# Bringing four experts' results back as two float32r parts in two rounds of products

## The chip, the cores and the metric

The kernel runs on one core of a Trainium2 chip. The metric is the device time of one execution in microseconds (us), lower is better. A program that runs on one core has its five engines work side by side: PE multiplies matrices (PEld in a profile is its loading of weights, which overlaps), DVE and ACT do elementwise work, POOL does some elementwise work and issues the indirect transfers, and SP issues the other transfers. Each engine, and each queue of transfers, goes through its own instructions in the order of the program and waits on semaphores for the others.

## The reference

The input is 16 sequences (b) of 512 tokens with 128 features. Six blocks follow one another, each added to x:

```python
x = x + 0.5 * L0_ffn(layernorm(x))     # a small network per feature
x = x + L0_attn(layernorm(x))          # causal attention, 16 heads of width 8
x = x + 0.5 * L0_ffn(layernorm(x))
x = x + 0.5 * L1_ffn(layernorm(x))     # experts, first pass: k=0
x = x + L1_attn(layernorm(x))          # a linear recurrence over the tokens
x = x + 0.5 * L1_ffn(layernorm(x))     # experts, second pass: k=1
```

The expert block is what the change touches. Each of 8 experts picks the 128 tokens of a sequence that score highest for it, runs them through two products with a gelu between, multiplies each row by that token's gain g, and adds the rows to the tokens that they came from:

```python
scores = einsum('ntd,ed->nte', x, gate_w)
g, m = top_k(softmax(scores).transpose(0, 2, 1), 128)    # gains and tokens, per sequence and expert
h = gelu(einsum('nekd,edf->nekf', x[batch, m], w1))      # 128 x 512 per sequence and expert
h = einsum('nekf,efd->nekd', h, w2)                      # 128 x 128
out = zeros_like(x).at[batch, m].add(g[..., None] * h)   # back to the tokens
```

## The kernel before

The kernel is one long program for all 16 sequences. The order on PE, ACT, DVE and POOL is written out by hand: Python generators each emit a few instructions and yield, and one main loop steps them. One step of that loop is called a turn. `turn()` emits what stands in the list `later` (work that was put off by one turn, mostly reads of a product's result), then steps the generators in `urgent` and `sides`. Until about 960 us the turns go through the attention of the sequences; in the background run the L0 networks.

Then `experts()` becomes the main generator. It goes through a list `order` of 256 jobs, a job being one expert's 128 tokens of one sequence in one of the two passes k. In the same turns there run in the background: `fetch` (POOL gathers a job's 128 rows with an indirect transfer xg, L864), `dispatch` (PE transposes two jobs at a time into ps_x, L888, ACT or DVE copies them to xin, L890), `recurrences` (two sequences at a time: norm with L286 to L303 and ps_t L317, ps_f L1051, ps_l L1060, ps_u L1070, scans L1074, ps_h L1090, and the scores ps_g L749), `routing` (picking 128 tokens of 512 for 64 rows at once: 16 rounds of three DVE instructions, L795 to L799), and `back`.

Results go back in two ways. Experts 0 to 3 of every sequence, and all eight of the last sequence in the last pass, go by products: 132 jobs. The other 124 go by transfer. `order` takes the jobs by products and the jobs by transfer alternately, the latter at a distance of some jobs behind, so that a sequence's four jobs by transfer come after its four jobs by products.

The loop keeps the last four jobs in `line`; each round of the loop emits something for each of them and has three yields, so a job takes three turns. For a job:

- In its own round, PE makes the hidden values ps_h (L939, four float32 products of 128 columns, which the profile shows as eight instructions) and ACT takes the gelu (L941) into one of four slots `hs`.
- One round later (`line[1]`), PE makes ps_y (L954, again eight instructions) and ACT multiplies by the gains (L957).
- For a job by products, DVE makes `sels` (L951), a 128x512 matrix in bfloat16 with a one where a row's token number equals the column. The scaled result is split into three bfloat16 parts whose sum is the float32 value: `yes[..0]` by ACT (L957), the remainder `rest` in float32 by DVE (L963), `yes[..1]` by ACT one round later (L945), `yes[..2]` by DVE (L960).
- Three rounds later (`line[3]`), PE multiplies the selection with the parts: for each of the four chunks of 128 tokens, three products of 128 columns into `acc` (L972), which is one bank of PSUM and collects four jobs. After the fourth, one add on DVE (L976) puts the bank on x[b], and one transfer on SP writes x[b] to a place in memory, `sums[k, b]` (L982).
- For a job by transfer, the scaled result stands in `ye`, and two rounds after its own (`line[2]`) POOL issues an indirect transfer that adds the rows to `sums[k, b]` in memory (L986). After a sequence's last one, `back` waits 18 turns and reads the sum back into x[b] (L923) for the recurrence, or copies it to the output in the last pass (L928). In the first pass it counts the sequence as done 9 turns later, and a pair of done sequences lets the next recurrence begin.

The tiles `mo` and `ye` are two buffers of 20 KB per partition that the attention no longer needs; the slots named above are cut from them.

Of the kernel before, what the change touches and what calls it, by code (L numbers as in the profile page):

```python
# [8 lines left out]
F32 = mybir.dt.float32  # L9
U32 = mybir.dt.uint32  # L10
BF16 = mybir.dt.bfloat16
F16 = mybir.dt.float16
AF = mybir.ActivationFunctionType
ALU = mybir.AluOpType
AX = mybir.AxisListType

P = 128
S = 512
NT = S // P
D = 128  # L20
# [11 lines left out]
E = 8  # L32
# [6 lines left out]
EP = 4  # L39
# [7 lines left out]
def tile_macaron(  # L47
# [9 lines left out]
    nc = tc.nc  # L57
    B = x_in.shape[0]
# [5 lines left out]
    x = []  # L64
# [34 lines left out]
    with ExitStack() as ph:  # L99
# [796 lines left out]
        def experts():  # L896

            mo = ptp.tile([P, 10, S], F32, name="mo", tag="pt")
            hs = [mo[:, i, :].rearrange("p (f j) -> p f j", f=NF) for i in range(4)]

            rest = [mo[:, 4, bass.ts(i, D)] for i in range(4)]

            def half(i, dtype):
                return mo[:, i // 2, i % 2 * (S // 2) : (i % 2 + 1) * (S // 2)].bitcast(dtype)

            sels = [half(14 + i, BF16) for i in range(4)]
            yes = [half(i, BF16)[:, 0 : 3 * D].rearrange("p (i d) -> p i d", i=3) for i in (12, 13, 18, 19)]  # L910

            iota = half(10, F16)
            nc.gpsimd.iota(mo[:, 6, :], pattern=[[1, S]], base=0, channel_multiplier=0,
                           allow_small_or_imprecise_dtypes=True)
            nc.gpsimd.tensor_copy(iota, mo[:, 6, :])
            ye = ptp.tile([P, 10, S], F32, name="ye", tag="pt")
            sums, line, acc = {}, [None] * 4, None
# [12 lines left out]
            while begun[0] < len(order) or any(line):  # L930
                now = None
                if begun[0] < moved[0]:
                    i = begun[0]
                    now = order[i] + (i % 4,)
                    k, b, e, u = now
                    begun[0] += 1
                    pst = scp.tile([P, NF, CAP], F32, name="ps_h", tag="ps_sc")
                    for f in range(NF):
                        nc.tensor.matmul(pst[:, f, :], lhsT=mw1[e][:, bass.ts(f, P)],  # L939
                                         rhs=xins[i // E % 2][:, i % E, :], start=True, stop=True)  # L940
                    nc.scalar.activation(hs[u], pst, AF.Gelu)  # L941
                prod = [work is not None and by_product(*work[:3]) for work in line]
                if prod[2]:
                    u = line[2][-1]
                    nc.scalar.copy(yes[u][:, 1, :], rest[u])  # L945
                yield
                if line[1]:
                    k, b, e, u = line[1]
                    g, n = b // GB, (b % GB) * E + e
                    if prod[1]:  # L950
                        nc.vector.tensor_scalar(sels[u], iota, tokT[g][:, n : n + 1], None, ALU.is_equal)  # L951
                    py = stp.tile([CAP, D], F32, name="ps_y", tag="ps_st")
                    for f in range(NF):
                        nc.tensor.matmul(py, lhsT=hs[u][:, f, :], rhs=mw2[e][:, f, :],  # L954
                                         start=(f == 0), stop=(f == NF - 1))
                    yu = yes[u][:, 0, :] if prod[1] else ye[:, b % 2 * (E - EP) + e - EP, 0:D]
                    nc.scalar.activation(yu, py, AF.Copy, scale=gainT[g][:, n : n + 1])  # L957
                if prod[2]:
                    v = line[2][-1]
                    nc.vector.tensor_sub(yes[v][:, 2, :], rest[v], yes[v][:, 1, :])  # L960
                yield
                if prod[1]:
                    nc.vector.scalar_tensor_tensor(rest[u], in0=py, scalar=gainT[g][:, n : n + 1],  # L963
                                                   in1=yes[u][:, 0, :], op0=ALU.mult, op1=ALU.subtract)
                if prod[3]:
                    k, b, e, u = line[3]
                    last = E - 1 if (k, b) == (1, B - 1) else EP - 1
                    if e == 0:
                        acc = avp.tile([P, NT, D], F32, name="acc", tag="ps_av")
                    for c in range(NT):  # L970
                        for w in range(3):
                            nc.tensor.matmul(acc[:, c, :], lhsT=sels[u][:, bass.ts(c, P)], rhs=yes[u][:, w, :],  # L972
                                             start=(e == 0 and c == 0 and w == 0), stop=(e == last and w == 2),
                                             skip_group_check=True)
                    if e == last:
                        nc.vector.tensor_add(x[b], acc, x[b])  # L976
                        if last < E - 1:
                            sums[k, b] = tc.dram_tile([S, D], F32, name=f"sum{k}_{b}")
                            to = sums[k, b].rearrange("(c p) d -> p c d", p=P)
                        else:  # L980
                            to = out[b].rearrange("(c p) d -> p c d", p=P)
                        nc.sync.dma_start(out=to, in_=x[b])  # L982
                if line[2] and not prod[2]:
                    k, b, e, u = line[2]
                    g, n = b // GB, (b % GB) * E + e
                    nc.gpsimd.indirect_dma_start(  # L986
                        out=sums[k, b], out_offset=bass.IndirectOffsetOnAxis(ap=tokI[g][:, n : n + 1], axis=0),
                        in_=ye[:, b % 2 * (E - EP) + e - EP, 0:D], in_offset=None, compute_op=ALU.add,
                    )
# [252 lines left out]
```

## Time and profile before

| | |
|---|---|
| median of 4 runs | 1663.89 us |
| lowest and highest | 1659.38, 1667.8 us |
| the profiled execution | 1667.7 us |
| its span in the profile | 1665.9 us |
| granted clock of PE over the span | 0.981 |
| PE busy | 1552.2 us (93%) |
| PE weight loads busy | 1078.3 us (65%) |
| DVE busy | 1136.3 us (68%) |
| ACT busy | 1001.9 us (60%) |
| POOL busy | 1021.7 us (61%) |
| products of L972 | 1584, 117.3 us busy |
| adding transfers of L986 | 124, 201.5 us busy on POOL |

The span runs from the first instruction of the program to the last; the execution's own time is 1.8 us longer. Matmuls are pipelined, so the mean duration of one is longer than its distance from the next, and the chain of waits, which follows the end of the program back through whatever released each step, gives the price of one more. A share of busy time is an average over stages with different limits, so stages are read one by one. POOL's time for an indirect transfer is that of issuing it; the transfer itself follows.

### The profile page before, as it was taken

Reading aid. Unit: us, or ns where it says so; the run is one execution under the profiler, and the core shown is the slowest. Engines: PE = TensorE matmul, PEld = TensorE weight load, DVE = VectorE, ACT = ScalarE, POOL = GpSimd, SP = SyncE. Lnnn points to the kernel's source line nnn. Section 1 sums busy time; section 2 is a strip of 40 time slices with the busy share of each in tenths; the row PEclk is TensorE's granted clock in tenths of the full one; section 3 lists DMA queues with packets and bytes.
Section 4 is the critical chain, followed back from the end, with each engine's and each line's share of the span. In section 5 each row is a group of like instructions: output and inputs, shape, how many; then the busy total and the mean of one; then the engine's idle time right before and its main releaser. Section 6 shows DMA issues by size and latency. Waiting matters only on the chain.

```text
span 1665.9 us, 35158 instructions
## 1 busy us (share of the span) xinstructions
PE 1552.2 (93%) x12813; PEld 1078.3 (65%) x12813; DVE 1136.3 (68%) x3616; ACT 1001.9 (60%) x2016; POOL 1021.7 (61%) x1486
## 2 busy tenths in 40 slices
PE   5689999999999999999989899999999999999998
PEld 2234445445444444454544489989988999889998
DVE  6588878888888888889987235964479555842222
ACT  3346677787778776777776754444443454444444
POOL 2634556556755665556543757667765777767774
PEclk9779999999999999999999999999999999999999
DMA  4110110111101110111122123223323333333332
GB/s 126 65 65 24 53 57 30 39 47 57 43 33 41 57 52 17 46 58 42 33 80 72 30 47 73 62 58 74 69 63 66 68 73 67 66 64 66 74 68 55
DMA packets 103253, 94.91 MB, mean 57 GB/s; under 512 B 13230, under 2 KB 91639, under 8 KB 102839
## 3 DMA queue, kind: packets, MB, share of 16 engines
q1 hardware_dynamic: 76220, 67.72, 13.1%
q0 software_dynamic: 26048, 24.93, 9.4%
q8 instruction: 101, 1.65, 0.4%
q14 instruction: 74, 0.60, 0.1%
q10 hardware_dynamic: 810, 0.02, 0.0%
HBM read 59.07 MB, written 37.49 MB: 58 GB/s over the span
## 4 chain that ended last, share of the span: by engine, by line
PE 69%; DVE 18%; ACT 4%; issue 3%; POOL 3%; DMA 1%; SPq 0%; DVEq 0%; ACTq 0%; POOLq 0%
PE ps_h L939 12%; PE ps_y L954 12%; PE ps_av L696 7%; PE ps_st L673 6%; PE ps_sc L610 6%; DVE below L615 5%; PE acc L972 5%; PE ps_kg L364 3%; PE ps_s L337 3%; PE ps_t L317 3%; DVE ln_st L286 2%; ACT pt L676 2%; PE ps_x L888 2%; PE ps_ko L385 2%; PE ps_g L749 1%
## 5 line engine op out<-in xcount | busy, mean ns | idle before, releaser
L678 POOL TENSOR_SCALAR_AFFINE_SELECT pt<-pt 128x128 f32<-128x128 f32 (+2 forms) x704 | 252.5, 366 | 327.9 <-ACT pt L676 323.1
L676 ACT ACTIVATE pt<-ps_st 128x512 f32<-128x512 f32 x682 | 368.2, 563 | 94.9 <-PE ps_st L673 89.2
L615 DVE CUSTOM_DVE_ANT_0 below<-ps_sc,causal 128x512 bf16<-128x512 f32 (+1 forms) x512 | 315.7, 617 | 80.2 <-PE ps_sc L610 64.9
L941 ACT ACTIVATE mo<-ps_h 128x512 f32<-128x512 f32 x256 | 152.7, 597 | 247.0 <-PE ps_h L939 134.0
L864 POOL DMA_INDIRECT xg<-xnd,tokI x256 | 250.5, 979 | 77.0 <-issue 45.2
L939 PE MATMUL ps_h<-xin,mw 128*128 128x128 f32 x2048 | 279.8, 279 | 0.8 <-issue 0.5
L954 PE MATMUL ps_y<-mw,mo 128*128 128x128 f32 x2048 | 274.6, 276 | 4.5 <-DVE mo L963 2.7
L610 PE MATMUL ps_sc<-kp,qp 72*128 72x512 bf16 (+3 forms) x1024 | 260.2, 306 | 11.7 <-DVE maxs L615 6.6
L673 PE MATMUL ps_st<-qp,kp 99*128 99x512 bf16 x992 | 250.7, 304 | 16.8 <-ACT pt L676 16.2
L986 POOL DMA_INDIRECT sum<-ye,tokI x124 | 201.5, 1625 | 90.6 <-ACT ye L957 39.7
L939 PEld LDWEIGHTS ps_h<-xin,mw 128*128 128x128 f32 x2048 | 251.4, 193 | 7.4 <-issue 6.1
L954 PEld LDWEIGHTS ps_y<-mw,mo 128*128 128x128 f32 x2048 | 250.9, 192 | 8.1 <-DVE mo L963 3.4
L673 PEld LDWEIGHTS <-kp 99*128 99x128 bf16 x1024 | 94.7, 100 | 177.1 <-issue 159.6
L370 ACT ACTIVATE kan_h<-kan_s,rbias,kw 128x512 f32<-128x512 f32 x256 | 205.9, 813 | 4.8 <-PE ps_kg L364 4.8
L696 PE MATMUL ps_av<-pt,va 128*32 128x512 f32 (+3 forms) x2048 | 164.6, 439 | 0.0
L620 DVE TENSOR_REDUCE maxs<-ps_sc 128x2 f32<-128x512 f32 (+1 forms) x192 | 130.3, 686 | 35.2 <-PE ps_sc L610 34.8
L610 PEld LDWEIGHTS <-qp 72*128 72x128 bf16 x1024 | 96.6, 100 | 79.9 <-issue 57.3
L960 DVE TENSOR_TENSOR mo<-mo 128x128 bf16<-128x128 f32 x132 | 38.4, 291 | 139.0 <-ACT mo L945 116.8
L972 PE MATMUL acc<-mo 128*128 128x128 bf16 x1584 | 117.3, 220 | 12.7 <-ACT mo L945 5.7
L972 PEld LDWEIGHTS <-mo 128*128 128x128 bf16 x1584 | 101.4, 99 | 31.2 <-issue 29.8
L696 PEld LDWEIGHTS ps_av<-pt,va 128*32 128x32 f32 x2048 | 53.5, 109 | 93.6 <-issue 43.1
L293 POOL TENSOR_TENSOR ln_rstd<-ln_rstd,mhalf 128x4 f32<-128x4 f32 x96 | 101.0, 1052 | 8.0
(194 smaller groups left out, 2341.3 us busy)
## 6 DMA issues: line engine op xcount, KB each, us to landing
qp<-qs SPq DMA_DIRECT2D x64, 288.0 KB
xnd<-kan_x SPq DMA_DIRECT2D x32, 256.0 KB
sum<-x SPq DMA_DIRECT2D x31, 256.0 KB
qs<-qpart SPq DMA_DIRECT2D x48, 128.0 KB
kp<-ks SPq DMA_DIRECT2D x48, 96.0 KB
x<-in_L_attn_x_dram SPq DMA_DIRECT2D x16, 256.0 KB
mw<-in_L_ffn_w_dram SPq DMA_DIRECT2D x16, 256.0 KB
xg<-xnd,tokI POOLq DMA_INDIRECT x256
```

Of the source, the lines that this page charges most:

```text
L370: nc.scalar.activation(h, sk[half], AF.Relu, bias=rbias[:, half, v : v + 1], scale=kw1[:, half, v : v + 1])
L610: nc.tensor.matmul(v[:, u, 0:n], lhsT=qp[r][0 : 9 * HD, g, bass.ts(c, P)], rhs=kp[0 : 9 * HD, r, 0:n], start=alone, stop=(u == len(gs) - 1 ...
L615: nc.vector.tensor_tensor_reduce(below[:, 0:n], v[:, 0, 0:n], causal[:, S - n : S], 1.0, LOWEST, ALU.add, ALU.max, accum_out=maxs[:, c, h ...
L673: nc.tensor.matmul(v[:, u, 0:n], lhsT=kp[ROWS, r, bass.ts(c, P)], rhs=qp[r][ROWS, g, c * P : S], start=True, stop=True)
L676: nc.scalar.activation(o, v[:, :, 0:n], AF.Exp, scale=HD ** -0.5)
L678: nc.gpsimd.affine_select(out=dg, in_=dg, compare_op=ALU.is_ge, fill=0.0, base=0, pattern=[[0, len(gs)], [1, P]], channel_multiplier=-1)
L696: nc.tensor.matmul(po[32 * g : 32 * g + 32, c * P : S], lhsT=va[:, c, r, :], rhs=pt[:, g, OFF[c] : OFF[c] + n], start=(c == 0), stop=(c == ...
L864: nc.gpsimd.indirect_dma_start(out=xgs[i // E % 2][:, i % E, :], out_offset=None, in_=xnd[b], in_offset=bass.IndirectOffsetOnAxis(ap=tokI[ ...
L939: nc.tensor.matmul(pst[:, f, :], lhsT=mw1[e][:, bass.ts(f, P)], rhs=xins[i // E % 2][:, i % E, :], start=True, stop=True)
L954: nc.tensor.matmul(py, lhsT=hs[u][:, f, :], rhs=mw2[e][:, f, :], start=(f == 0), stop=(f == NF - 1))
L972: nc.tensor.matmul(acc[:, c, :], lhsT=sels[u][:, bass.ts(c, P)], rhs=yes[u][:, w, :], start=(e == 0 and c == 0 and w == 0), stop=(e == las ...
L986: nc.gpsimd.indirect_dma_start(out=sums[k, b], out_offset=bass.IndirectOffsetOnAxis(ap=tokI[g][:, n : n + 1], axis=0), in_=ye[:, b % 2 * ( ...
```

## The change

The jobs by products no longer use three bfloat16 parts. The result is kept as two parts in float32r, a 4-byte type that PE takes in place of float32: the value as ACT writes it in that type, and the remainder as DVE writes it. The selections are float32r too. The products of four experts are no longer spread over their four rounds of the loop: when the fourth job has come to `line[3]`, two entries are put on the list `rounds`, and each round of the loop takes one. Such a round makes one half of the tokens (two chunks): for each chunk and each of the four experts one product of 256 columns, 128 for each of the two parts, into a bank that is laid out as chunk, part, feature. In the next turn DVE adds the two parts to that half of x[b], one after the other, and SP writes that half to memory.

The cast L945 and the subtraction L960 go away. Selections and parts have eight slots instead of four; the float32 results of the jobs by transfer move to another tile, and two buffers of the attention's pool `va` take some of the parts. A job by transfer now issues its adding transfer at `line[3]`, one round later than before. For the last sequence in the last pass, eight jobs go by products in two groups of four, and only the second group writes the output.

```diff
+            sels = [ye[:, i, :] for i in range(2 * EP)]
+            added = [mo[:, 4 + i // 4, bass.ts(i % 4, D)] for i in range(2 * (E - EP))]
+            more = [vap.tile([P, S], F32R, name=f"parts{i}", tag="va") for i in range(2)]
+            parts2 = [(ye[:, 8 + i // 2, :] if i < EP else more[i // 2 - EP // 2])[:, bass.ts(i % 2, 2 * D)]
+                      .rearrange("p (w d) -> p w d", w=2) for i in range(2 * EP)]
...
+            def combine(k, b, group, h):
+                acc = avp.tile([P, 2, 2, D], F32, name="acc", tag="ps_av")
+                slots = [place[k, b, e] for e in range(group * EP, (group + 1) * EP)]
+                for j in range(2):
+                    for i, u in enumerate(slots):
+                        nc.tensor.matmul(acc[:, j, :, :], lhsT=sels[u][:, bass.ts(2 * h + j, P)], rhs=parts2[u],
+                                         start=(j == 0 and i == 0), stop=(i == EP - 1), skip_group_check=True)
+                last = group == (1 if (k, b) == (1, B - 1) else 0)
+                if last and h == 0 and not group:
+                    sums[k, b] = tc.dram_tile([S, D], F32, name=f"sum{k}_{b}")
+                def close():
+                    mine = x[b][:, 2 * h : 2 * h + 2, :]
+                    for w in range(2):
+                        nc.vector.tensor_add(mine, acc[:, :, w, :], mine)
+                    if last:
+                        to = (out[b] if group else sums[k, b]).rearrange("(c p) d -> p c d", p=P)
+                        nc.sync.dma_start(out=to[:, 2 * h : 2 * h + 2, :], in_=mine)
+                later.append(close)
...
-                if prod[2]:
-                    u = line[2][-1]
-                    nc.scalar.copy(yes[u][:, 1, :], rest[u])
...
-                if prod[2]:
-                    v = line[2][-1]
-                    nc.vector.tensor_sub(yes[v][:, 2, :], rest[v], yes[v][:, 1, :])
...
-                    nc.vector.scalar_tensor_tensor(rest[u], in0=py, scalar=gainT[g][:, n : n + 1],
-                                                   in1=yes[u][:, 0, :], op0=ALU.mult, op1=ALU.subtract)
+                    nc.vector.scalar_tensor_tensor(parts2[v][:, 1, :], in0=py, scalar=gainT[g][:, n : n + 1],
+                                                   in1=parts2[v][:, 0, :], op0=ALU.mult, op1=ALU.subtract)
...
-                    for c in range(NT):
-                        for w in range(3):
-                            nc.tensor.matmul(acc[:, c, :], lhsT=sels[u][:, bass.ts(c, P)], rhs=yes[u][:, w, :],
-                                             start=(e == 0 and c == 0 and w == 0), stop=(e == last and w == 2),
-                                             skip_group_check=True)
-                    if e == last:
-                        nc.vector.tensor_add(x[b], acc, x[b])
...
-                        nc.sync.dma_start(out=to, in_=x[b])
-                if line[2] and not prod[2]:
-                    k, b, e, u = line[2]
+                    if e % EP == EP - 1:
+                        rounds.extend((k, b, e // EP, h) for h in range(2))
+                if rounds:
+                    combine(*rounds.pop(0))
+                if line[3] and not prod[3]:
+                    k, b, e, u = line[3]
```

More of the change, by code (lines that the diff above doesn't have):

```diff
@@ L12 @@
 F16 = mybir.dt.float16
+F32R = mybir.dt.float32r
 AF = mybir.ActivationFunctionType
@@ L901, in experts @@
             mo = ptp.tile([P, 10, S], F32, name="mo", tag="pt")
+            ye = ptp.tile([P, 10, S], F32R, name="ye", tag="pt")
             hs = [mo[:, i, :].rearrange("p (f j) -> p f j", f=NF) for i in range(4)]
[L904 to L910, printed above, removed]
@@ L912, in experts @@
-            iota = half(10, F16)
-            nc.gpsimd.iota(mo[:, 6, :], pattern=[[1, S]], base=0, channel_multiplier=0,
-                           allow_small_or_imprecise_dtypes=True)
-            nc.gpsimd.tensor_copy(iota, mo[:, 6, :])
-            ye = ptp.tile([P, 10, S], F32, name="ye", tag="pt")
-            sums, line, acc = {}, [None] * 4, None
+            sels = [ye[:, i, :] for i in range(2 * EP)]
+            added = [mo[:, 4 + i // 4, bass.ts(i % 4, D)] for i in range(2 * (E - EP))]
@@ new lines, in experts @@
+            more = [vap.tile([P, S], F32R, name=f"parts{i}", tag="va") for i in range(2)]
+            parts2 = [(ye[:, 8 + i // 2, :] if i < EP else more[i // 2 - EP // 2])[:, bass.ts(i % 2, 2 * D)]
+                      .rearrange("p (w d) -> p w d", w=2) for i in range(2 * EP)]
+            iota = mo[:, 6, 0 : S // 2].bitcast(F16)
+            nc.gpsimd.iota(mo[:, 7, :], pattern=[[1, S]], base=0, channel_multiplier=0,
+                           allow_small_or_imprecise_dtypes=True)
+            nc.gpsimd.tensor_copy(iota, mo[:, 7, :])
@@ new lines, in experts @@
+            sums, line = {}, [None] * 4
+            place = {job: i % (2 * EP) for i, job in enumerate(products)}
+            rounds = []
+            def combine(k, b, group, h):
[16 more added lines that the diff above has]
+                later.append(close)
@@ L928, in back @@
                     nc.sync.dma_start(out=out[b], in_=sums.pop((k, b)))
-            while begun[0] < len(order) or any(line):
+            while begun[0] < len(order) or any(line) or rounds:
                 now = None
@@ L950, in experts @@
                     if prod[1]:
-                        nc.vector.tensor_scalar(sels[u], iota, tokT[g][:, n : n + 1], None, ALU.is_equal)
+                        v = place[k, b, e]
+                        nc.vector.tensor_scalar(sels[v], iota, tokT[g][:, n : n + 1], None, ALU.is_equal)
                     py = stp.tile([CAP, D], F32, name="ps_y", tag="ps_st")
@@ L955, in experts @@
                                          start=(f == 0), stop=(f == NF - 1))
-                    yu = yes[u][:, 0, :] if prod[1] else ye[:, b % 2 * (E - EP) + e - EP, 0:D]
+                    yu = parts2[v][:, 0, :] if prod[1] else added[b % 2 * (E - EP) + e - EP]
                     nc.scalar.activation(yu, py, AF.Copy, scale=gainT[g][:, n : n + 1])
-                if prod[2]:
-                    v = line[2][-1]
-                    nc.vector.tensor_sub(yes[v][:, 2, :], rest[v], yes[v][:, 1, :])
@@ L966, in experts @@
                     k, b, e, u = line[3]
-                    last = E - 1 if (k, b) == (1, B - 1) else EP - 1
-                    if e == 0:
-                        acc = avp.tile([P, NT, D], F32, name="acc", tag="ps_av")
-                    for c in range(NT):
-                        for w in range(3):
-                            nc.tensor.matmul(acc[:, c, :], lhsT=sels[u][:, bass.ts(c, P)], rhs=yes[u][:, w, :],
-                                             start=(e == 0 and c == 0 and w == 0), stop=(e == last and w == 2),
-                                             skip_group_check=True)
@@ L975, in experts @@
-                    if e == last:
-                        nc.vector.tensor_add(x[b], acc, x[b])
[L977 to L981, printed above, removed]
-                        nc.sync.dma_start(out=to, in_=x[b])
-                if line[2] and not prod[2]:
-                    k, b, e, u = line[2]
+                    if e % EP == EP - 1:
+                        rounds.extend((k, b, e // EP, h) for h in range(2))
@@ L987, in experts @@
                         out=sums[k, b], out_offset=bass.IndirectOffsetOnAxis(ap=tokI[g][:, n : n + 1], axis=0),
-                        in_=ye[:, b % 2 * (E - EP) + e - EP, 0:D], in_offset=None, compute_op=ALU.add,
+                        in_=added[b % 2 * (E - EP) + e - EP], in_offset=None, compute_op=ALU.add,
                     )
```

## The prediction

> **What bounds the kernel now.** I read the page first, then the time by stages, then in each stage the chain of waits.
>
> ```profile
> PE   5689999999999999999989899999999999999998
> ...
> DVE  6588878888888888889987235964479555842222
> ```
>
> Each digit is a slice of 42 us. The expert loop starts near 960 us; from there PE is full, and DVE is full only around 1040, 1230 to 1290 and 1430 to 1470 (the k=1 routing). The next view gives busy time of PE, PEld, DVE, ACT, POOL by stage.
>
> ```profile
> 1232.00:1290.00 58.00, 52.74 (x448) 48.38 (x448) 56.25 (x187) 22.81 (x58) 34.04 (x33) 0.94 0.28 59
> ...
> 1470.00:1640.00 170.00, 163.65 (x1616) 159.44 (x1614) 46.40 (x138) 74.61 (x192) 122.92 (x105) 1.00 0.35 68
> ```
>
> In the first stage DVE is busy 56.25 of 58 us: it sets the pace. In the second PE does. The same windows for L972 alone count the matmuls that the change replaces; 48 are one group of four experts.
>
> ```profile
> 960.00:1053.00 93.00, 16.80 (x228) 14.47 (x228) 1.00 0.27 55
> 1053.00:1232.00 179.00, 26.14 (x372) 23.21 (x372) 1.00 0.34 69
> ...
> 1290.00:1431.00 141.00, 20.34 (x288) 17.99 (x288) 1.00 0.34 70
> ...
> 1470.00:1640.00 170.00, 31.95 (x424) 27.13 (x422) 1.00 0.35 68
> 1640.00:1666.00 26.00, 5.98 (x90) 5.30 (x86) 1.00 0.25 44
> ```
>
> So of 33 groups 4.75 lie in stage A (960 to 1053), 7.75 in B (1053 to 1232), 6 in D (1290 to 1431), 8.8 in F (1470 to 1640), 1.9 in the tail, and the other 4 in the routing stages C and E. The chain of waits (start, duration, what) shows what a pair of jobs, one by products and one by transfer, costs:
>
> ```profile
> 1059.34 0.86 PE ps_l L1060 x2
> ...
> 1080.62 1.69 PE ps_g L749 x16
> ...
> 1644.13 0.67 PE acc L972 x12
> 1644.80 0.95 PE ps_h L939 x8
> 1645.75 0.89 PE ps_y L954 x8
> 1646.64 0.89 PE ps_h L939 x8
> 1647.53 0.89 PE ps_y L954 x8
> ```
>
> Only PE stands in these last five rows. The pair takes 4.29 us, and 4.51 with two transposes ps_x (0.22 on the chain). POOL is close behind; this is its order in stage F (start, duration, idle before):
>
> ```profile
> 1587.52 1.62 POOL L986 DMA_INDIRECT sum<-ye,tokI  x1 [0.30 <-issue]
> 1589.44 0.98 POOL L864 DMA_INDIRECT xg<-xnd,tokI  x1 [0.30 <-PE ps_y L954]
> 1590.73 0.95 POOL L864 DMA_INDIRECT xg<-xnd,tokI  x1 [0.31 <-issue]
> 1591.99 1.62 POOL L986 DMA_INDIRECT sum<-ye,tokI  x1 [0.30 <-issue]
> ```
>
> One adding transfer and two gathers, back to back with 0.30 us between, repeat every 4.47 us. POOL is called 72% busy, yet has no more than 0.04 us to spare per pair.
>
> **The products on PE.** Before, a group takes 4 x 0.67 = 2.68 us, and each burst makes the next ps_h 0.95 instead of 0.89: 2.92 us. After, it is 16 instructions of 256 columns, in two rounds of 8. The trace shows no float32r, so I bound one. From below: the bf16 burst streams 128 columns in 0.67/12 = 0.056 us, so 256 in 0.112; a 128x128 float32 weight load paces ps_g's rows of 8 columns at 1.69/16 = 0.106 and would just hide under that. From above: float32 ps_l takes two instructions per product, each 0.43 us for 512 columns: 0.215 us for 256 in one pass, 0.43 in two. I take 0.112, nearest to the bf16 burst, because a float32 product is four times that burst's price (two instructions, each at half its column rate) and float32r asks for one rounded number in place of high and low parts. The group is then 16 x 0.112 = 1.79 us and saves 1.13 us, 0.28 us per pair.
>
> The Trainium skill ("FP8 and Floating Point Precision", TensorE Precision Notes) has true FP32 as four passes and a reduced FP32 that is read in 4 bytes and cut to FP22; a quarter of float32's 0.43 would be 0.108 us an instruction and 1.73 us a group. Against the change speaks "TensorE: Matmul & The Clock Gate", Weight-path perf modes: fast weight load is only for inputs that aren't FP32. In this trace a lone bf16 load is 99 ns and a float32 one 193 ns on the mean; where such loads didn't overlap, an instruction would be 0.106 + 0.112 and the group 3.5 us, which is the second rival's sum.
>
> **Removed parts.** ACT's cast L945 (132 x 0.293 us) and DVE's subtraction L960 (132 x 0.291) go. ACT is 44% busy in F, so its share earns nothing by itself. But PE waited for those two before acc 14 times, 8.3 us in all. Both parts are now ready two jobs before their products, so this wait goes; I count 2 us in A, the rest lies inside F or in C and E, where DVE is late next.
>
> **DVE.**
>
> ```profile
> L951 DVE TENSOR_SCALAR mo<-mo,tokT 128x512 bf16<-128x512 f16 x122 | 44.4, 364 | 0.0
> ...
> L1066 DVE TENSOR_SCALAR lam<-lam 128x512 f32<-128x512 f32 x8 | 4.1, 517 | 5.6 <-issue 3.8 <-ACT lam L1062 1.0 <-ACT ye L957 0.8
> ...
> L777 DVE TENSOR_TENSOR probs<-probs,sm 128x256 f32<-128x256 f32 x3 | 1.3, 424 | 0.1
> ```
>
> These groups give mean ns after the busy time. The selection in 4-byte float32r goes from 364 ns towards L1066's 517: +0.13 to +0.15 us each; at worst it costs what the 128x512 add L976 does on the chain, 0.60 in place of 0.25, +0.35. The 128x512 add of 0.69 us (0.60 on the chain) becomes four of 128x256, 0.42 each (0.33 back to back: 1.33). Per group on DVE's chain: -4 x 0.19 for L960, +4 x 0.13, +0.73, so +0.49 us, at worst +1.37. Only C and E (4 groups) pay: +2 us, at worst +5.5. Elsewhere PE's four float32 bursts per pair hide it.
>
> **The two rounds share one bank.** Round two waits for the two adds of round one. Between them PE has the next job's ps_h and ps_y, 1.78 us, against 0.85 us of adds: hidden, unless DVE is over 0.9 us late. Behind a late round two stand the next ps_h and its gelu. The longest runs ahead of an add are two scans L1074 (2.47 us) and eight ln_st (1.54), in B and D where DVE is 59% and 53% busy. I put +2 us in all; the ends are 0 and 1.5 us for each of those 13.75 groups, +21. The new half writes are two SP issues of 0.36 us for one; SP issues little here, and both land four jobs before the first transfer that needs them, so nothing.
>
> **Transfers one step later.** On POOL the adding transfer, with its tail of gathers, no longer stands waiting for ACT's ye, which it did 25 times for 39.7 us in all (2.2 us at 1529). What is queued behind it, two gathers and the rstd pair of a norm, moves up. The read-back, the recurrences and the k=1 gathers come one job (2.2 us) later in program order; the shortest lead of a gather over its transpose is 7.1 us against 2.6 us from issue to use, which covers it. What is late next in F is POOL's own 4.47 us: 35 pairs took 170 us (4.86 each), PE alone would allow 4.51 - 0.28 = 4.23, POOL allows 4.47. So F falls to 156.4, -13.6 us (PE alone: 148, -22).
>
> **Sum.** A -(4.75 x 1.13) - 2 = -7.4; B -8.8; C and E +2; D -6.8; F -13.6; tail -(1.9 x 1.13) = -2.1, and its last chain: before 3.92 us from the last ps_y to the last add's end, after 0.38 + 0.36 + 0.9 + 0.85 + 0.9 + 0.85 = 4.24, +0.3; shared bank +2. Together -34.4 us. The profiled execution took 1667.7 us (span 1665.9), so 1633.3; it lies 3.8 us above the median of 1663.9, and on that the sum is 1629.5. I say 1630, 2% less.
>
> **Rivals.**
>
> One: the saving is eaten by the shared bank. DVE over half busy in B and D speaks for it, 1.78 us of cover against it. With 1 us lost in each of 20 groups outside F and the routing stages: -14, 1650.
>
> Two: float32r streams like one float32 pass, 0.215 us. Group 3.44, +0.52. A +0.5, B +4.0, C and E +2, D +3.1, tail +1.9, F 35 x (4.51 - 0.73 + 0.86) = 162.4, -7.6, bank +2: +5.9, 1670. For it: every float32 row of the trace runs at this rate.
>
> Three, slower: float32r is run as plain float32, so the change's lighter product isn't there: two instructions of 0.215 for 256 columns. Group 6.88, +3.96: A +17, B +31, C and E +10, D +24, tail +11, F 35 x 5.50 = 192.5, +22.5, bank +2: about +117, 1781. It decides from 2.92/16 = 0.183 us per product of 256 columns upwards. For it: all 4-byte products in this trace are such pairs.
>
> **How the numbers follow.** The forecast has 0.66, rival one 0.10, two 0.10, three 0.14. A measurement of this kernel can tell 0.5%, 8.3 us, from no change. Faster: 0.66 + 0.07 of rival one = 0.73; within: 0.03 + 0.07 of rival two = 0.10; slower: 0.03 + 0.14 = 0.17. The forecast's own range is 1613 (F at PE's floor, no stall left) to 1645 (DVE and bank at half of their worst). With rivals one and two it reaches 1672, leaving out rival three and a little at each end.
>
> **What would show it.** Right: 528 products in the acc row at about 0.11 us on the chain, none over 0.13; in F a pair of 4.3 to 4.5 us with POOL back to back and hardly a wait on ye; C and E as long as before. Wrong: 0.2 us or more per product, or 1056 of them; waits of the second round for x's adds over 10 us in all; F still over 4.7 us a pair.

## The result, and the profile after

The changed kernel takes 1668.91 us (median), the kernel before 1663.48 us in the runs beside it: ratio 1.0029, 95% interval 1.0020 to 1.0037. It is slower by 0.3%, where 2% less was forecast. The profiled execution took 1671.07 us, its span is 1669.3.

Busy tenths in 40 slices, from the page of the changed kernel:

```profile
PE   5689999999999999999999999999997999889988
...
DVE  6588878888888888889987246955588555842323
```

In the slices from 1252 to 1294 us and from 1419 to 1502 us PE now shows 7 and 8 tenths, where it was at 9: it has less to do, and stands. The time by stages (PE, PEld, DVE, ACT, POOL busy, then the granted clock) of the changed kernel:

```profile
1431.00:1470.00 39.00, 32.60 (x254) 31.95 (x255) 36.32 (x91) 14.38 (x33) 24.75 (x21) 0.91 0.33 59
1470.00:1640.00 170.00, 156.03 (x1316) 152.06 (x1315) 51.73 (x131) 70.29 (x156) 123.71 (x104) 0.98 0.35 68
```

From 1470 to 1640 us PE is busy 7.6 us less than before, and by the starts of the jobs nothing goes faster there. In the stage above it the granted clock is 0.91, where it was 1.00. The products are nearly as cheap as forecast; this is a round in the chain of waits of the changed kernel (start, duration, what):

```profile
1597.52 0.95 PE acc L926 x8
```

A round of eight takes 0.95 us and a group 1.90, and the next ps_h is back at 0.89; before it was 2.92 in all, so TensorE is spared some 1.0 us in each of 33 groups. What it waits for now, in the waits of PE from 950 us on (us in all, times, longest):

```profile
PE acc L926 <- DVE x L935: 11.6, 7, 3.5
PE ps_t L318 <- DVE kan_x L304: 11.3, 12, 3.7
PE ps_x L889 <- DMA xg<-xnd,tokI: 4.4, 2, 4.0
```

Second rounds wait for additions, the norm's transposes for kan_x, the transposes of gathered rows for their gathers. By the starts of the 256 jobs the changed kernel is 1.7 us ahead at job 0 and 9.1 us ahead at job 104, then loses 9.7 us up to job 184 (1253 to 1485 us, where the second pass's routing lies), and gains nothing after it. From job 184 to job 248 a pair takes 4.91 us, before 4.85; from job 192 to job 255 it takes 4.71, before 4.77.

### The profile page after: what moved, and what is told of

It is laid out like the page before. It is cut to its first block, busy times and chain, and to the rows that moved or that the text cites. A ratio compares the mean times of both kernels' runs of the same rounds, so it can differ in the third digit from the quotient of the medians.

```text
span 1669.3 us, 32926 instructions
## 1 busy us (share of the span) xinstructions
PE 1533.9 (92%) x11757; PEld 1057.6 (63%) x11757; DVE 1154.6 (69%) x3584; ACT 984.6 (59%) x1884; POOL 1023.6 (61%) x1486
## 4 chain that ended last, share of the span: by engine, by line
PE 67%; DVE 20%; ACT 5%; issue 4%; POOL 4%; DMA 1%; another core or an unknown queue 0%; DVEq 0%; SPq 0%; ACTq 0%; POOLq 0%
PE ps_y L975 11%; PE ps_h L962 11%; PE ps_av L697 7%; PE ps_st L674 6%; PE ps_sc L611 6%; DVE below L616 5%; PE acc L926 4%; PE ps_kg L365 3%; PE ps_s L338 3%; PE ps_t L318 3%; DVE ln_st L287 2%; ACT pt L677 2%; PE ps_ko L386 2%; PE ps_g L750 1%; PE ps_x L889 1%
## 5 line engine op out<-in xcount | busy, mean ns | idle before, releaser
L975 PE MATMUL ps_y<-mw,mo 128*128 128x128 f32 x2048 | 278.0, 280 | 6.1 <-ACT mo L978 2.5
L962 PE MATMUL ps_h<-xin,mw 128*128 128x128 f32 x2048 | 274.9, 277 | 3.4 <-ACT mo L964 3.4
L975 PEld LDWEIGHTS ps_y<-mw,mo 128*128 128x128 f32 x2048 | 255.4, 196 | 8.7 <-ACT mo L978 3.2
L992 POOL DMA_INDIRECT sum<-mo,tokI x124 | 203.5, 1641 | 85.9 <-issue 27.6
L935 DVE TENSOR_TENSOR x<-acc,x 128x256 f32<-128x256 f32 x132 | 55.9, 423 | 66.1 <-PE acc L926 49.0
L318 PE MATMUL ps_t<-ident,kan_x 128*128 128x128 f32 x384 | 68.7, 297 | 34.3 <-DVE kan_x L308 20.8
L365 PE MATMUL ps_kg<-kan_h,w2d 128*32 128x512 f32 x512 | 86.1, 656 | 0.9 <-ACT kan_h L371 0.8
```

Source lines behind the costliest of these rows:

```text
L992: nc.gpsimd.indirect_dma_start(out=sums[k, b], out_offset=bass.IndirectOffsetOnAxis(ap=tokI[g][:, n : n + 1], axis=0), in_=added[b % 2 * ( ...
```

## The experiments

Some names in the expectations need saying. *Theory 1*: the second rounds, which wait for additions, give the saving back. *Theory 2*: the later adding transfers do. *Theory 3*: POOL's pace does. After the first four runs theory 2 was split: *theory A*, the later step lengthens the loop of the second layer (adding transfers, read-back, recurrence, scores, routing, gathers); *theory B*, it only changes POOL's order.

The kernel before took 1665 to 1668 us beside the first eight runs (other chips) and 1639 to 1640 beside the last ten. So a ratio is compared within its own set, and sets of the same level with each other. Runs 4, 13 and 14 leave a part of the sums out, so they show a time and no usable kernel.

| | kernel | median us | ratio to before, 95% |
|---|---|---|---|
| 1 | before, transfers one step later | 1681.47 | 1.0085 (1.0055 to 1.0116) |
| 2 | changed, transfers at the old step | 1659.45 | 0.9960 (0.9937 to 0.9983) |
| 3 | changed, one job more between the rounds | 1686.70 | 1.0131 (1.0102 to 1.0160) |
| 4 | before, two of three products | 1649.67 | 0.9914 (0.9885 to 0.9944) |
| 5 | 1, read-back one job earlier | 1667.40 | 1.0013 (0.9993 to 1.0033) |
| 6 | before, transfers later in the second pass only | 1667.06 | 1.0005 (0.9984 to 1.0025) |
| 7 | 2, first round one job earlier | 1656.40 | 0.9953 (0.9930 to 0.9976) |
| 8 | 2, products of 128 columns, one round | 1694.05 | 1.0158 (1.0122 to 1.0195) |
| 9 | changed, read-back one job earlier | 1637.77 | 0.9981 (0.9967 to 0.9996) |
| 10 | before, read-back one job earlier | 1639.80 | 1.0001 (0.9987 to 1.0014) |
| 11 | 7, transfers later, read-back earlier | 1641.30 | 1.0000 (0.9988 to 1.0013) |
| 12 | 11, rstd two turns later | 1639.11 | 0.9991 (0.9977 to 1.0004) |
| 13 | before, half the adding transfers | 1637.46 | 0.9988 (0.9976 to 1.0000) |
| 14 | 2, half the adding transfers | 1625.64 | 0.9917 (0.9903 to 0.9930) |
| 15 | before | 1639.00 | 1.0000 (0.9986 to 1.0014) |
| 16 | 2 again | 1642.42 | 1.0017 (1.0000 to 1.0034) |
| 17 | 1 again | 1646.11 | 1.0039 (1.0026 to 1.0052) |
| 18 | the changed kernel again | 1651.13 | 1.0073 (1.0053 to 1.0092) |

### The two halves of the change, each alone (1, 2, 17, 18)

Runs 1 and 17 make this one edit in the kernel before; runs 2 and 16 take it out of the changed kernel:

```diff
-                if line[2] and not prod[2]:
-                    k, b, e, u = line[2]
+                if line[3] and not prod[3]:
+                    k, b, e, u = line[3]
```

> The kernel before, with nothing changed but that the adding transfers are given out one step later (three bfloat16 parts and 48 products a group as before). Theory 1 (the new second round is what gives the saving back: its products wait for the additions of the first round, which stand on VectorE behind the next product job's work): within 3 us of the kernel before, 1661 to 1667. Theory 2 (the later transfers give it back: the read-backs and half-writes that wait on SyncE behind them come later, and POOL with them): slower by 5 us or more, 1668 to 1680. Theory 3 (POOL with its gathers and its share of the norms sets the pace, so TensorE's saving can't be had at all): within 3 us, and POOL's waits on the scaled results, 39.7 us before, fall to under 15.

> The changed kernel with the adding transfers given out where they were before (one step earlier); everything else as changed. Theory 1: about as long as the changed kernel, 1665 to 1672, and the same single waits of about 3 us ahead of second rounds. Theory 2: well below the kernel before, 1645 to 1658. Theory 3: as the changed kernel, 1665 to 1672.

The later step alone costs 0.85%, 14 us; without it the changed products are 0.4% below before. Theory 2 has the sign of both, though each time lies 1.5 us above the range that it gave. The last set, on a chip where before takes 1639 us, repeats it:

> The first experiment once more (before, with the adding transfers one step later). Theory A, the later step costs through the loop of the second layer whatever the chip: 0.5 to 1.0% over before, with POOL's waits for ln_mv 10 us or more above those of before. If the first result needed the stalls of its chip: within 0.3% of before.

> The changed kernel once more, beside the first experiment's edit on the same chip. If the parts add (later step 0.5 to 1.0%, cheaper products between -0.4 and +0.2% by the second and the sixteenth): 0.2 to 0.9% over before.

There the later step costs 0.39%, 7 us, in the kernel before, less than the 0.5% that theory A asked for. The changed kernel is 0.73% above before and its twin with early transfers 0.17% (run 16): 0.56% between them. The parts add within their intervals. POOL's waits for ln_mv grew less than expected of run 17, from 44.1 to 49.8 us; theory A's price is elsewhere, as the next part shows.

### Why a step later costs (5, 6, 10, 9)

```diff
             def back(k, b):
-                for _ in range(18):
+                for _ in range(15):
                     yield
```

> The kernel of the first experiment (before, with the adding transfers one step later), with the read-back of a batch given out three turns, that is one job, earlier after its last transfer (15 turns instead of 18), so that it leaves at the same job as in the kernel before. The first experiment took 0.85% more than before. Theory A (the later step costs through the loop of the second layer: the later read-back of x makes the norms, the scores and the second routing late, and with them the gathers that wait for the routing): the cost goes, 1661 to 1669, and POOL's waits for VectorE ahead of rstd, 63.2 us in the first experiment and 48.8 before, are back under 53 us. Theory B (it costs through POOL's order: the transfers now stand behind other gathers and rstd): no change, 1676 to 1684.

Run 6 issues the transfers of pass k=0 at `line[2]` and those of k=1 at `line[3]`:

> The kernel before, with the adding transfers one step later only for the second layer's jobs (k = 1), whose read-back goes to out and lets no norm begin; the first layer's transfers stay where they were. Theory A (loop of the second layer): within 4 us of before, 1661 to 1670, plus at most one job at the very end (2.4 us). Theory B (POOL's order): half or more of the 14 us, 1670 to 1677, lost in the last 170 us.

Both take the cost away: 1.0013 and 1.0005, against 1.0085 on another chip of the same level. The transfers stand as late in POOL's order in run 5 as in run 1, so the order isn't it (theory B falls); only the first pass matters, whose read-back lets the recurrence begin. POOL's waits for ln_mv are 52.0 us in run 5, against 63.2 in run 1.

How one job becomes microseconds is seen at the change of passes. Rows of DVE and of POOL (start, duration, idle before) in run 15, the kernel before:

```profile
1219.76 0.68 DVE L786 COPY wk<-ps_p 64x512 f32<-64x512 f32 x1
...
1277.83 0.20 DVE L815 CAST tokI<-ps_r 128x64 uint32<-128x64 f32 x1
```

```profile
1273.13 0.98 POOL L864 DMA_INDIRECT xg<-xnd,tokI  x1 [0.30 <-PE ps_x L888]
...
1282.35 1.04 POOL L864 DMA_INDIRECT xg<-xnd,tokI  x1 [0.31 <-issue]
```

The same rows in run 17, with the transfers later, and what PE waited for at that place:

```profile
1223.28 0.67 DVE L786 COPY wk<-ps_p 64x512 f32<-64x512 f32 x1
...
1280.55 0.18 DVE L815 CAST tokI<-ps_r 128x64 uint32<-128x64 f32 x1
```

```profile
1272.65 0.95 POOL L864 DMA_INDIRECT xg<-xnd,tokI  x1 [0.30 <-issue]
...
1285.29 1.04 POOL L864 DMA_INDIRECT xg<-xnd,tokI  x1 [0.30 <-issue]
```

```profile
PE ps_x L888 <- DMA xg<-xnd,tokI: 3.4, 1, 3.4
```

Up to the routing both kernels are level (job 104 starts at 1242.5 and 1242.0). The selection starts 3.5 us later, with 99 jobs begun instead of 98, because its scores come one job later; tokI is ready 2.7 us later. In both kernels 123 gathers are out by then, and the next one needs tokI. At this place tokI isn't what it waits for last: tokI stands at 1278.0 and 1280.7 us, and POOL comes to the gather 4.3 and 4.6 us after that. Ahead of it in POOL's order are two rstd pairs and a transfer, and before the first rstd POOL waits 3.4 and 4.9 us for ln_mv, which DVE makes behind the selection. So the late selection reaches the gathers through the orders of DVE and POOL. From the last gather before the stop to the first after it 9.2 us pass in run 15 and 12.6 in run 17; PE uses up what has been gathered and waits 3.4 us, where it waited 1.2. Job 128 then starts 5.5 us late: PE also waits 1.0 us for the routing's own product, and after the 3.4 us its granted clock is 0.50 from 1288.1 to 1291.4 us. At the second routing the gather does wait for tokI, 4.1 us, where run 15 waits 1.2 for gainT beside it; job 184 starts 6.9 us late, and run 17 stays 6.9 us late to the end.

> The kernel before with the same number altered (15 turns instead of 18) and the transfers where they were, so that the read-back leaves one job earlier than ever. If the loop of the second layer is what bounds the kernel before, one job less in it gains what one job more cost (14 us): 1648 to 1657. If the loop only costs when it is made longer (the work before it is covered by something else, TensorE and POOL): 1661 to 1667.

In the kernel before the loop is just covered: a job less of it gains nothing (1.0001), a job more costs. So in the changed kernel the same number should give back what its later step took:

> The changed kernel with one number altered: a batch's read-back leaves 15 turns after its last transfer instead of 18, so that it leaves at the same job as in the kernel before. By theory A (the later transfers cost through the loop read-back, norms, scores, routing, gathers) the changed kernel gets back what its later step costs: 1650 to 1659, 0.3 to 0.8% below before. If its 0.3% came from its second rounds instead: 1664 to 1670.

It does: 0.9981 against run 18's 1.0073, 0.9% on chips of the same level. It is the one version with all of the work whose interval lies below before there, by 0.2%, less than expected.

Run 9 also lies 0.36% below run 16 (0.9981 and 1.0017, intervals that don't meet, two chips of the same level), and the two differ only in the later transfers with the read-back in time. So the later step has a good side, which the longer loop hides: from 1480 to 1600 us PE waits 3.7 us for gathers in run 9 and 6.2 in run 16, and a pair (jobs 184 to 248) takes 4.44 us and 4.55.

### The rounds, and the bank they share (3, 7, 11, 8)

```diff
-                        rounds.extend((k, b, e // EP, h) for h in range(2))
+                        rounds.extend([(k, b, e // EP, 0), None, (k, b, e // EP, 1)])
...
```

> The changed kernel with the second round of each group one job later still, so that two jobs of TensorE work lie between the rounds instead of one. Theory 1: the waits of the products for VectorE's additions, 11.6 us in the changed kernel, fall under 3 us, and the time by 6 to 12 us, to 1657 to 1663. Theory 2: no gain (the second half of the sum is written a job later, which makes the queue on SyncE no shorter): 1667 to 1673. Theory 3: those waits fall, but what is saved turns into waits for POOL: 1666 to 1670.

No theory had foreseen 1.0131. The wait moved to POOL: the second half of a sum is written a job later, too late for the first transfer that adds to it. POOL's waits in run 3:

```profile
POOL sum L993 <- DMA sum<-x: 37.6, 9, 6.0
```

Run 7 has the same gap but starts the first round at `line[2]`, so that the sum is written no later; it also has early transfers:

> The second experiment (changed products, transfers at their old step, 0.4% below before) with the first round of products one job earlier and the second where it is, so that a whole job lies between them and the additions of the first round have two jobs of TensorE work over them, while the sum is written no later. Theory 1 (what is left of TensorE's saving is eaten by second rounds that wait for additions, 8.7 us in the stages after 1290 us): these waits fall under 2 us and the time to 1646 to 1655. Theory 3 (POOL sets the pace, 4.47 us for two gathers and one transfer back to back): 1656 to 1662, with POOL's waits on scaled results no longer falling.

PE's waits for additions fell from 9.8 us (run 2) to 1.5, but the earlier first round now waits for its parts: all waits of acc together fell from 12.7 us to 7.6. The time fell from 0.9960 to 0.9953 of before, far inside the intervals of 0.23% either way, and lies in theory 3's range. So theory 1 names a real wait, and its range is missed; that the bank costs a few us is not ruled out.

> The best so far, the seventh (changed products, rounds a whole job apart), with the transfers one step later and the read-back at 15 turns: all parts of the change, each without what it was found to cost. POOL's waits for scaled results, 23 us in the seventh, should shrink and the first 100 jobs gain some 3 us more. If the gains add: 1647 to 1655, below the seventh (1656.4, 0.47% below before); if POOL's pace bounds both: 1654 to 1660.

Its chip gives 1.0000, so neither gain is there. It differs from run 9 beside it (0.9981) only in the rounds; the waits for additions fell from 7.2 us to 1.1, 4.3 us of waits for parts came up, and nothing was gained. What seemed the best on the first chips isn't on these.

Run 8 splits each product in two and needs one round, one bank and one addition:

```diff
+                        for w in range(2):
+                            nc.tensor.matmul(acc[:, c, :], lhsT=sels[u][:, bass.ts(c, P)], rhs=parts2[u][:, w, :],
...
```

> The second experiment with the products of 256 columns split into two of 128 that add both parts into the same 128 columns: 32 products a group into one bank, one round instead of two, one addition of 0.69 us instead of four of 0.42. If a float32r product costs by its columns (0.06 us for 128), a group takes 32 x 0.06 = 1.9 us as now, VectorE is given back 4 x 0.42 - 0.69 = 0.99 us a group, no second round waits, and the time falls to 1645 to 1655. If a product of 128 columns takes as long as one of 256 (0.12) or runs at the float32 rate (0.215), a group takes 3.8 or 6.9 us, and the time is 1675 to 1700 or over 1720.

The chain of waits of run 8:

```profile
1509.20 3.53 PE acc L927 x32
```

A float32r product of 128 columns takes 3.53/32 = 0.110 us, one of 256 took 0.119, and the 1694 us lie in the range given for this. So the 256 columns, and the bank they fill, are needed for the low price.

### Where TensorE's saving goes (4, 13 to 16, 12)

Run 4 leaves the third part's products out of the kernel before (`range(2)` for `range(3)` over w):

> The kernel before, with the products of the third bfloat16 part left out (32 products a group instead of 48; the third part is still made, and the sum lacks it). It takes 16 x 0.061 = 0.97 us of TensorE work out of each of 33 groups, 32 us in all, and adds no wait, no bank shared in turn and no work on VectorE. Theory 1 and theory 2: the saving can be had, so the time falls by 15 to 25 us, to 1638 to 1649. Theory 3: hardly anything comes of it, 1657 to 1664, and TensorE's waits for gathers and for norms grow by about what was saved.

By the ratio it gains 14 us of 16 x 33 x 0.056 = 30. That is just short of the range of theories 1 and 2 and more than theory 3 allowed, so POOL's pace alone doesn't hold the saving up on this chip; still half of the plainest saving is lost, with no round and no bank in it. It was not repeated on a chip where before takes 1639 us. Runs 13 and 14 then take work off POOL:

```diff
+                    if e % 2:
                         nc.gpsimd.indirect_dma_start(
...
```

> The kernel before without the adding transfers of experts 4 and 6 (their results are still made, but not added to the sum): POOL's work falls from two gathers and one transfer a pair (4.47 us back to back) to 2.57 + 0.97 us on the mean. Theory 3 (POOL's pace bounds what TensorE saves; before, both are about equally late): 3 to 10 us under before, since TensorE's own work stays. If POOL alone bounds before: 15 us or more under it. If POOL never mattered: within 2 us.

> The second experiment (changed products, transfers at their old step) without the adding transfers of experts 4 and 6, as in the thirteenth. Theory 3: with POOL out of the way TensorE's saving is had, 15 to 28 us under the thirteenth. Theory 1 (second rounds wait for additions) or VectorE as the bound: 3 to 10 us under the thirteenth, as far as the two lie apart with all transfers.

> The kernel before itself, for its profile on the same chip as the two others: ratio 1.000 within 0.002; a job pair after 1480 us takes 4.5 us if TensorE is stalled as little as in the tenth experiment, 4.85 us if it is stalled as in the first profile.

> The second experiment once more, on the chip of the two others: again 0.2 to 0.6% under before if its gain doesn't depend on the chip; within 0.1% of before if it does, as the eleventh experiment (no gain on its chip) lets one suspect.

All four ran on one chip. With all transfers the cheaper products bring nothing (run 16, +0.17%, so the gain of run 2 depends on the chip); with half of them 11.8 us (run 14 against 13), between the ranges of theory 3 and of its rivals. So the left-out transfers hold back about 14 us of TensorE's saving (11.8 and the 2.3 by which run 16 lies over before). Run 13 alone gains 2.6 us, a little less than theory 3 said: before, POOL isn't the bound. Leaving transfers out also empties their queue and lets read-backs go earlier; that it is POOL's own time is shown for the stretch from 1480 to 1600 us alone (PE, PEld, DVE, ACT, POOL busy; runs 15, 16 and 14 in this order):

```profile
1480.00:1600.00 120.00, 120.00 (x1228) 119.70 (x1227) 34.02 (x100) 59.50 (x146) 93.29 (x80) 1.00 0.37 73
```

```profile
1480.00:1600.00 120.00, 113.77 (x996) 111.58 (x995) 37.28 (x93) 53.78 (x117) 92.54 (x79) 1.00 0.37 72
```

```profile
1480.00:1600.00 120.00, 120.00 (x1071) 120.00 (x1070) 38.89 (x99) 58.03 (x127) 71.72 (x64) 1.00 0.30 68
```

Before, PE has no gap at all. With cheaper products it stands 6.2 of 120 us, all of it for gathers (run 16, same stretch):

```profile
PE ps_x L889 <- DMA xg<-xnd,tokI: 6.2, 9, 1.6
```

With half the transfers it is full again, and a pair (starts of jobs 184 to 248) takes 4.27 us; the other three take 4.51 (run 15), 4.55 (run 16) and 4.51 (run 13). POOL's own order in run 18 has no gap but the 0.30 us between two instructions:

```profile
1499.43 0.98 POOL L865 DMA_INDIRECT xg<-xnd,tokI  x1 [0.30 <-issue]
...
1501.98 1.62 POOL L992 DMA_INDIRECT sum<-mo,tokI  x1 [0.30 <-ACT mo L978]
1503.90 0.98 POOL L865 DMA_INDIRECT xg<-xnd,tokI  x1 [0.30 <-issue]
```

That is 4.47 us a pair, and the changed kernel's pair takes 4.45 there (jobs 184 to 248).

> The eleventh with POOL's two operations of rstd given out two turns later in the last stages (the norm after it keeps its turn), so that POOL, which takes its work in order, issues gathers and transfers while VectorE still makes ln_mv; POOL waited 50 us for ln_mv in the seventh. Theory 3 (POOL's waits in its order hold the gathers up): those waits fall under 20 us and the time by 4 to 10 us against the eleventh. If POOL's waits cost nothing: within 3 us of the eleventh. If the norm then waits for rstd: slower by 2 to 6 us, with TensorE's waits for kan_x above 15 us.

The waits for ln_mv fell only from 41.7 to 37.5 us, so run 12 doesn't decide (0.9991, overlapping run 11). Computing rstd on VectorE, which would free POOL of it, was not run.

## Why the prediction was wrong, step by step

**The price of a float32r product** was right in kind. 0.112 us was forecast; a round takes 0.95/8 = 0.119 on the chain. By starts, the median distance within a round is 0.120 us; the first of each round takes about 0.20, and after some stalls a round runs at the halved clock told of below. Rivals two and three, with 0.215 or more for every product, are out. Why the products cost so little no run here shows. A group takes 1.90 us, not 1.79, so the saving is 1.0 us, not 1.13. A pair on TensorE alone takes 4.27 us (run 14), 4.23 forecast.

**DVE's prices** were right: the selection takes 492 ns and an addition 423 on the mean in the changed kernel (L972 and L935, from 1000 to 1660 us); 0.50 and 0.42 stood in the sum.

**The transfers one step later** is the step that failed. It was booked at -13.6 us in F, its later read-back at nothing, and together it costs 7 to 14. The read-back was put at nothing by a reading that is wrong: "the shortest lead of a gather over its transpose is 7.1 us" doesn't hold for the profile of before. At the change of passes a gather leads its transpose by 2.59 us (1293.87 to 1296.46), and PE already waits for it. The chain of waits of that profile runs there from the selection and ln_mv on DVE over POOL to the transposes (start, duration, what; its last pieces):

```profile
1289.02 0.24 POOL ln_rstd L292
...
1291.91 1.65 POOL sum L986
...
1293.87 2.33 DMA xg<-xnd,tokI
...
1296.46 0.33 PE ps_x L888
```

2.59 us is the time from issue to use and no more, so there was no lead to cover a job of 2.2 us. The next least lead is 2.69 us, at 1098.9 us, behind the routing before. At these places the gathers are stopped until the routing is made, and the later read-back made it one job later. In the changed kernel, which reaches the routing earlier, the loop costs more: jobs 104 to 184 take 14.0 us longer in run 18 than in run 16 and 12.8 longer than in run 9, against 7.4 in the kernel before (run 17 against 15). The good side that was booked is there and small: run 18's pair in F takes 4.45 us against run 16's 4.55, and POOL's waits for ye, 39.7 us, are 25.2 in the changed kernel (slots of mo now), not next to nothing. The half writes, booked at nothing because they land four jobs early, did stop POOL twice, for 9.8 us (longest 7.4): a read-back that waits for later transfers stands ahead of them in SP's order.

**F falls to POOL's 4.47 us** was about right as a floor (run 9 takes 4.44, run 18 4.45) and wrong as a gain. The 4.86 us a pair in the profile of before weren't the kernel's pace. On other chips the same program takes 4.51, which is the chain's own sum in the prediction, with PE 120.00 us busy of 120. The rest of the 4.86 was 0.35 us a pair of single stalls on the first chip, which the prediction put down to POOL's waits on ye and let the change remove. It removed hardly any: there F takes 4.91 us a pair after, or 4.71 over the last 63 jobs, where before takes 4.77. Where before runs free, F had 4.51 - 4.47 = 0.04 us a pair to give, 1.4 us of the 13.6; and the prediction had this number, "no more than 0.04 us to spare per pair".

**A and B** were booked at -16.2 us; the profile shows -7.4 (jobs 0 to 104). POOL was thought of in F alone, but easing it helps here too: in these jobs run 14, with half the transfers, gains 6.9 us on run 15, run 18, with later transfers, 5.5, and run 16, with neither, 1.5. The 9 us still missing are not fully explained. Part is the norm: PE waits for kan_x 3.0 us there in run 14, where it had not waited for it in run 15. kan_x comes behind rstd on POOL, and PE now comes earlier; that this is the reason is argued, not shown.

**The shared bank** was booked at +2 us, and its waits are 11.6 us, over the 10 that the prediction gave as the sign of being wrong. Rival one, which priced this at -14 us of gain left, had the right wait. Its weight is not settled: taking most of the wait away brought new waits for parts and moved the time by 0.07% (run 7 against run 2, two chips of the same level), and not at all in run 11 against run 9.

**C, D and E** were booked at -4.8 us and lost 9.7. In run 18 jobs 104 to 184 take 15.3 us longer than in run 15. By runs 16 and 9 the later step with its read-back accounts for 13 to 14 of them. They show as such waits, run 18's PE from 1219 to 1470 us, where before had 8.1 us in all:

```profile
PE ps_t L318 <- DVE kan_x L304: 8.9, 7, 3.7
PE ps_x L889 <- DMA xg<-xnd,tokI: 6.9, 3, 4.0
PE acc L926 <- DVE x L935: 6.3, 2, 3.6
```

and in the granted clock (the third figure from the end), which the sum left out. The same stretch in runs 15 and 18:

```profile
1219.00:1470.00 251.00, 242.59 (x2274) 226.99 (x2273) 173.41 (x562) 117.26 (x280) 180.14 (x166) 1.00 0.33 67
```

```profile
1219.00:1470.00 251.00, 225.71 (x1784) 209.80 (x1783) 172.20 (x518) 103.98 (x217) 168.56 (x154) 0.96 0.30 62
```

The sum, then, on the chips where before takes 1639 us: TensorE is spared some 33 us. Run 14 has 11.8 of them against run 13, so about 21 are lost even with POOL eased and the transfers at their old step. There PE's waits are 8 us longer (17.7 against 10.0), and the clock is halved for 17.1 us, which costs up to 8.5 (an estimate, half of that time); the rest stays open. POOL's pace and the transfers take about 14 more, the later step about 9 (run 18 against 16). 33 - 21 - 14 - 9 is -11, and run 18 lies 12 us above before.

## What to carry to other kernels

Where two engines are within 1% of each other, a saving on one is worth that 1% until the other is eased; take work off the second for one run, even at the price of the result, to see what the first is worth. Before a step is moved later, follow its last consumer around every loop that the data makes, and take the least lead over the whole run, at the places above all where a queue is stopped by data: a wait that is already there says that no lead is left. Stalls in one profile are not a program's pace: set the sum of the chain's own rows against the pace, and don't book the difference as a gain unless the change removes what made it.

## What the runs showed of the hardware that was not expected

A float32r product costs nearly the same for 128 columns (0.110 us) as for 256 (0.119), and 0.119 is a little over a quarter of the two float32 instructions of 0.215 us that the same columns would take (an estimate from the 0.43 us of a float32 instruction of 512 columns).

A long wait of PE can cost more than itself. These are rows of PE in run 18 (start, duration, idle before); eight instructions of ps_y take 1.06 us in such a row otherwise:

```profile
1252.89 2.31 PE L318 MATMUL ps_t<-ident,kan_x 128*128 128x128 f32 x8 [3.66 <-DVE kan_x L304]
1254.99 1.92 PE L975 MATMUL ps_y<-mw,mo 128*128 128x128 f32 x8
```

From 1251.8 to 1258.5 us the granted clock is 0.50 there, and products start 213 ns apart instead of 112. Between job 0 and job 255 run 18 has 20.5 us at half clock in five stretches of 3.4 or 6.8 us, and run 15 has none; the changed kernel's first profile has eight stretches, 27.3 us, and before has two, 6.8 us. Two of the eight make the 0.91 shown above. Which waits do it these runs don't settle. In run 18 the clock fell by distances of 3.07, 3.85, 3.94 and 4.24 us between two starts, and not by 2.97 and 3.03; in the changed kernel's first profile it fell by 2.97 and not by 3.10 and 3.28. One of run 18's stretches, three of the eight and both of before have no distance above 2.1 us beside them. The Trainium skill ("TensorE: Matmul & The Clock Gate", Why this matters for your kernels) warns of idle gaps above about 3 us, after which the clock falls back to half; most of these rows agree, and the last two kinds do not.

The same program took 1.4 to 1.8% longer on some chips than on others, nearly all of it in the expert loop: job 0 starts at 954.1 and 952.7 us, job 248 at 1640.1 and 1611.7 (the first profile and run 15). The mean durations of the instructions are the same within about 1% (ps_h 279 and 278 ns, a gather 978 and 981); the slower traces show pauses of issue between them (from 1480 to 1600 us 5.6 us on PEld before the products and 6.3 us on DVE), the faster one none on these engines. What makes the pauses stays open.
